# Layer 2's mixing matrix S: one row part from 32-column matmuls, the other from the copies out of PSUM

## The chip, the cores and the metric

One Trainium2 chip, one core. The metric is the device time of the kernel in microseconds (us). TensorE's trace has two rows, PE for matmuls and PEld for weight loads; DVE is VectorE, ACT is ScalarE, POOL is GpSimd, SP is the engine that issues most DMAs.

## The reference

The input x has 16 samples of 16 channels of 256x256 fp32 pixels. Four layers follow each other, each of the form x = x + layer(groupnorm(x)): a circular 3x3 convolution, a 5x5 convolution with a diagonal kernel, a pole-residue layer, and a quantised 3x3 convolution. Only the third, layer 2, is touched:

```
alpha = fft2(x)
A  = 1 / (omega1 - weights_pole1)          Bm = 1 / (omega2 - weights_pole2)
S  = einsum('ikpq,oikp,xikq->oxik', weights_residue, A, Bm)
output_residue1 = einsum('biox,oxik->bkox', alpha, S)
x1 = real(ifft2(output_residue1))          # x2, a second term, comes from the same poles
return x1 + x2 / Nx / Ny
```

For every frequency pair (o, x) a complex 16x16 matrix S mixes the channels i of alpha into the channels k of the result. In real numbers that is a 32x32 matrix: the rows for the real part of alpha hold (Re S, Im S), the rows for the imaginary part hold (-Im S, Re S). These two groups of rows are the two row parts.

## The kernel before

The program runs in stages. Layers 0 and 1 take about the first 1,300 us. The next stage (to about 2,240 us) transforms each sample and stores alpha to DRAM (`alphad`). Then comes the stage of this document, about 2,240 to 3,100 us: S is made and multiplied with alpha, and the product goes to DRAM (`mixd`). The inverse transform (to about 3,970 us) reads `mixd`, and layer 3 ends the program.

In the mixing stage four frequencies o share one matmul. The tile `z` holds, on 128 partitions, the rows of alpha of four frequencies f, and in its columns a block for each f, zero elsewhere. The tile `sk` holds S for the same four: for each of 129 positions x a 128x32 stationary matrix. One product is `sk[:, x]` (128x32) against `z[:, :, x]` (128x64), written to one of four groups of 32 PSUM partitions (L958). Sixty-four rounds n (`NF`) of 129 products follow each other. In a round, the loop over `at` runs 32 times with four products each; every eighth `at` closes a PSUM tile `ps_m`, which ScalarE copies in part to `other` (L983) and VectorE adds and subtracts into `ob` (two operations recorded at the helper's line L190). `ob` is stored to `mixd` (`leave`, L911) and `z` for a later round is loaded from `alphad` (`load`, L907, sixteen partitions to a DMA), both on SP's queue.

`system(e8)` makes S for eight frequencies, two rounds' worth, in eight steps of two channels k. A step works through both halves h of the input channels. For each it multiplies `l` (`ls[h]`, 128x128: the factor A, masked; its columns are 8 frequencies, 2 row parts, 8 channels) with `t2[:, h, k]` (128x258: the sum over q of residue and Bm, the two parts interleaved with x) for two k into a tile `ps_s` (L891), and copies the two frequency halves n of that tile into two `sk` tiles, 64 partitions each, on ScalarE (L896). Thus a step is four matmuls and four copies. `masked` makes `l` on GpSimd, four operations for two steps; `poles` makes `af`, the factor A with both row parts, on GpSimd and VectorE once for eight steps.

The order of the work is written out by hand in this stage (`manual_schedule` for PE, DVE, ACT and POOL): the engines take their instructions in the order in which the code issues them. `next(steps)` issues one step at each eighth `at`, so a step and 32 products alternate, four times in a round. The eight steps of `system(0)` come before the first product; 248 of the 256 steps lie between products, and the last two rounds have none. `ps_s` has two buffers, `ps_m` three, `sk` four.

Of the kernel before, what the change touches and what calls it, by code (L numbers as in the profile page):

```python
# [57 lines left out]
P = 128  # L58
C = 16
# [12 lines left out]
def constants():  # L72
# [10 lines left out]
    def sin(a, b):  # L83
# [81 lines left out]
def layers(ctx, tc, x, w0, w1, w3, sw, bias, ty, tx, p1a, p1b, p1c, p2a, p2b, p2c, resa, resb,  # L165
# [23 lines left out]
    def tt(eng, o, a, b, op):  # L189
        eng.tensor_tensor(o, a, b, op)  # L190
# [368 lines left out]

    between = ExitStack()  # L560
    late2 = between.enter_context(tc.tile_pool(name="late2", bufs=1))
    t2 = new(late2, [HC, C, NX, 2], "t2")
# [5 lines left out]
    def sums_over_q(pool, psum):  # L568
# [32 lines left out]
        for h in range(HC):  # L601
            for k0 in range(0, C, KQ):
                e, g = new(pool, [KQ, NX], "qe"), new(pool, [KQ, NX], "qg")
                of = lambda c: bc(c[:, h, k0 : k0 + KQ], 2, NX)
                tt(Q, e, bc(wx, 1, KQ), of(pxi), SUB)
                nc.scalar.activation(g, e, AF.Square)
                tt(Q, g, g, of(px2), ADD)
                yield
                V.reciprocal(g, g)
                yield  # L610
                V.scalar_tensor_tensor(e, e, turn[:, 2:3], of(pxr), MUL, ADD)
                tt(V, e, e, g, MUL)
                w = new(pool, [2 * KQ, 2, 8, 8], "qw")
                c0 = h * C + k0
                for v in range(2):
                    tt(Q, w[:, :, v], bc(cf[:, c0 : c0 + KQ].rearrange("p n (m r) q -> p (n m) (r q)", m=2), 3, 8),
                       bc(bc(vi[:, v], 1, 8), 1, 2 * KQ), MUL)
                yield
                for k in range(KQ):
                    ps = psum.tile([P, 512], F32, tag="ps_a", name="ps_t")  # L620
                    for m in range(2):
                        nc.tensor.matmul(ps[:, m * NX : (m + 1) * NX], start=m == 0, stop=m == 1, rhs=e[:, k],
                                         lhsT=w[:, 2 * k + m].rearrange("p v r i -> p (v r i)"), skip_group_check=True)
                    nc.scalar.copy(t2[:, h, k0 + k].rearrange("p x r -> p r x"),
                                   ps[:, 0 : 2 * NX].rearrange("p (r x) -> p r x", r=2))
# [5 lines left out]
        Q.tensor_scalar(t2[:, :, :, 0, 0], t2[:, :, :, 0, 1], -1.0, None, MUL)  # L631
        Q.tensor_copy(t2[:, :, :, 0, 1], a)
        yield

    afs, lss, sks = {}, {}, {}
# [5 lines left out]
    def poles(e8, pool=None, psum=None):  # L641


        af = afs[e8] = new(head, [HC, 2, C, FC], f"af{e8 % 2}")
        if pool:
            e, d = new(pool, [HC, C, FC], "ae"), new(pool, [HC, C, FC], "ad")
        else:
            e, d = (new(head, [KC, FC, 2, 8], f"l{h}1").rearrange("p k f r i -> p (k f r i)")[:, 0 : HC * C * FC]
                    .rearrange("p (h k f) -> p h k f", h=HC, k=C) for h in range(HC))
        g = psum.tile([P, HC, C, FC], F32, tag="ps_g", name="ps_g") if psum else d  # L650
        for h in range(HC):
            tt(Q, e[:, h], bc(wy[:, FC * e8 : FC * e8 + FC], 1, C), bc(pyi[:, h], 2, FC), SUB)
        yield
        tt(Q, d, e, e, MUL)
        yield
        tt(Q, d, d, bc(py2, 3, FC), ADD)
        yield
        V.reciprocal(g, d)
        yield
        eng = V if psum else Q  # L660
        for k, at in enumerate(blocks):
            tt(eng, af[at, :, 1 - k % 2], e[at], g[at], MUL)
            yield
            tt(eng, af[at, :, k % 2], g[at], bc(pyr, 3, FC)[at], MUL)
            yield

    def masked(e8, k0):

        if e8 == NE:
            return  # L670
        ls = []
        for h in range(HC):
            l = new(head, [KC, FC, 2, 8], f"l{h}{k0 // KC % 2}")
# [3 lines left out]
            ls.append(l.rearrange("p k f r i -> p k (f r i)"))  # L677
        lss[e8, k0] = ls


    with ExitStack() as es:
# [77 lines left out]
        rows2 = alphad.rearrange("(p s) h r i q x b -> p s h r i q (x b)", s=2)  # L759
        es.enter_context(tc.manual_schedule(engines={mybir.EngineType.PE}))  # L760

        def quarters(b, g):
# [26 lines left out]
        def across(b, i, y, al, acc):  # L789
# [13 lines left out]
            V.scalar_tensor_tensor(flat(al[:, 1, :, :, b % BG]), pc, not0, sums[1], MUL, SUB)  # L803
            if b % BG == BG - 1:
                for s_, eng in enumerate((nc.sync, Q)):
                    eng.dma_start(rows2[:, s_, i // 8, :, i % 8, b // BG, :],
                                  al[:, s_].rearrange("p r x b -> p r (x b)"))

            ps = ps_d.tile([P, P], F32, tag="ps_d", name="ps_d")
# [56 lines left out]
    with ExitStack() as es:  # L866
# [12 lines left out]
        def system(e8):  # L879


            for n in range(2):
                sks[2 * e8 + n] = new(sp, [NX, 2 * C], "sk")
            for k0 in range(0, C, KC):
                masked(*((e8, k0 + KC) if k0 + KC < C else (e8 + 1, 0)))
                ls = lss.pop((e8, k0))
                for k in range(k0, k0 + KC, 2):
                    for h in range(HC):
                        ps = ps_s.tile([P, 2, 512], F32, tag="ps_s", name="ps_s")
                        for d in range(2):  # L890
                            nc.tensor.matmul(ps[:, d, 0 : 2 * NX], lhsT=ls[h][:, k + d - k0],  # L891
                                             rhs=t2[:, h, k + d].rearrange("p x r -> p (x r)"), start=True, stop=True)
                            if d:
                                for n in range(2):
                                    copy = V.tensor_copy if e8 == 0 and n and h else nc.scalar.copy
                                    copy(sks[2 * e8 + n][64 * h : 64 * h + 64, :, 2 * k : 2 * k + 4]  # L896
                                         .rearrange("p x (k r) -> p x k r", r=2),
                                         ps[64 * n : 64 * n + 64, :, 0 : 2 * NX].rearrange("p k (x r) -> p x k r", r=2))
                    yield

        PX = 32
        GX = 8

        def load(n, h, f, to):

            rows_ = slice(64 * h + 16 * f, 64 * h + 16 * f + 16)
            nc.sync.dma_start(zs[n % 2][rows_, 4 * to : 4 * to + 4].rearrange("p q x b -> p (q x b)"),  # L907
                              alphad[4 * n + f, h].rearrange("r i q x b -> (r i) (q x b)"))

        def leave(n, p_):  # L910
            nc.sync.dma_start(mixd[2 * n + p_].rearrange("t k r u b g -> (t k r) (u b g)"),  # L911
                              obs[n][:, p_].rearrange("p u b g -> p (u b g)"))

        def halfload(n, h):

            if n < NF:
                z = zs[n % 2]
                for f in range(4):
                    V.memset(z[64 * h : 64 * h + 64, 4 * f, 0, 0:1], 0.0)
                    load(n, h, f, f)  # L920

# [8 lines left out]
        for _ in range(3):  # L930
            next(coming)
        Q.memset(zs[0][:, FB // 2 :], 0.0)
        for h in range(HC):
            for f in range(4):
                for to in ((0, 1) if f < 2 else (f,)):
                    load(0, h, f, to)
        for at, _ in enumerate(system(0)):
            for _ in range(2):
                next(coming, None)
# [78 lines left out]
    with ExitStack() as es:  # L1018
# [99 lines left out]
        with tc.manual_schedule(engines={mybir.EngineType.PE}):  # L1118
            before = None
            exps = exponentials(0)  # L1120
            for k in range(0, C, 2):
                for b in range(B):
                    if b % BD == 0:

                        ot = op.tile([P, 2, 2, 4, 2, BD, 32], F32, tag="ot", name="ot")
                        for a in range(2):
                            for d in range(2):
                                for r in range(2):
                                    for u in range(2):
                                        nc.sync.dma_start(  # L1130
                                            ot[64 * u : 64 * u + 64, a, d, :, r].rearrange("p t b g -> p t (b g)"),
                                            mixd[64 * a : 64 * a + 64, :, k + d, (r + u) % 2, u, b : b + BD]
                                            .rearrange("q t b g -> q t (b g)"))
                    if b == 4:
                        coming = exponentials(k + 2) if k + 2 < C else None
# [271 lines left out]
```

## Time and profile before

| what | value |
|---|---|
| three timed runs | 4389.43, 4389.74 and 4402.79 us, median 4389.74 us |
| the profiled execution's own time, first to last instruction (its span) | 4393.6 us, 3.9 us over the median |
| PE busy over the span | 3976.0 us (90%) |
| DVE, ACT, POOL busy over the span | 69%, 63%, 48% |
| mixing with steps, from 2276 to 3069 us: PE, ACT, POOL, DVE busy of 793 us | 756, 668, 504, 420 us |
| DMA in that stretch | mean busy share 0.74, 167 GB/s |
| `z` loads, `mixd` stores: issues, KB each, median us to landing | 516, 129.0, 4.8; 128, 512.0, 5.9 |

Busy time of an engine is the time in which one of its instructions runs; matmuls are pipelined and their ends are modelled, so PE's share counts starts more safely than ends. A fp32 matmul shows as two instructions, so the 1,024 matmuls of S are 2,048 in the profile. An operation recorded through the helper at L190 is told apart by its tiles.

### The profile page before, as it was taken

Reading aid. Unit: us, or ns where it says so; the run is one execution under the profiler, and the core shown is the slowest. Engines: PE = TensorE matmul, PEld = TensorE weight load, DVE = VectorE, ACT = ScalarE, POOL = GpSimd, SP = SyncE. Lnnn points to the kernel's source line nnn. Section 1 sums busy time; section 2 is a strip of 40 time slices with the busy share of each in tenths; the row PEclk is TensorE's granted clock in tenths of the full one; section 3 lists DMA queues with packets and bytes.
Section 4 is the critical chain, followed back from the end, with each engine's and each line's share of the span. In section 5 each row is a group of like instructions: output and inputs, shape, how many; then the busy total and the mean of one; then the engine's idle time right before and its main releaser. Section 6 shows DMA issues by size and latency. Waiting matters only on the chain. (4 is left out here: it accounts for less than half of the span.)

```text
span 4393.6 us, 122873 instructions
## 1 busy us (share of the span) xinstructions
PE 3976.0 (90%) x50832; PEld 3066.8 (70%) x50832; DVE 3037.6 (69%) x5678; ACT 2753.7 (63%) x3699; POOL 2125.9 (48%) x3350
## 2 busy tenths in 40 slices
PE   5999999999958989899989999999799999996776
PEld 1555555555538989899977777777588888884444
DVE  4667677666668878787755555554477777768988
ACT  2877676868624434444458888888555544446998
POOL 2242323333245646564556666665476666663222
PEclk9999999999979999999999999999799999998999
DMA  6767676767443545344547777777788888877998
GB/s 147 168 166 181 156 184 148 192 143 193 111 124 115 164 133 164 121 159 150 169 89 163 164 172 167 172 174 166 209 228 235 231 244 234 244 219 257 357 351 306
DMA packets 481647, 820.57 MB, mean 187 GB/s; under 512 B 41728, under 2 KB 373504, under 8 KB 465664
## 3 DMA queue, kind: packets, MB, share of 16 engines
q1 hardware_dynamic: 433984, 644.64, 54.8%
q0 software_dynamic: 47104, 168.06, 12.8%
q8 instruction: 401, 6.57, 0.7%
q14 instruction: 158, 1.29, 0.1%
HBM read 408.85 MB, written 336.07 MB: 170 GB/s over the span
## 5 line engine op out<-in xcount | busy, mean ns | idle before, releaser
L382 PE MATMUL ps<-va,wt 128*64 128x512 f32 (+1 forms) x1632 | 667.8, 570 | 11.4 <-POOL va L354 9.2
L382 PE MATMUL ps<-vb,wt 128*64 128x512 f32 (+1 forms) x1632 | 666.0, 569 | 4.5 <-DMA vb<-va 4.5
L896 ACT COPY sk<-ps_s 64x516 f32<-64x516 f32 x1016 | 592.3, 583 | 115.6 <-PE ps_s L891 96.3
L786 ACT ACTIVATE y<-ps_y,bc 128x384 f32<-128x384 f32 x512 | 296.0, 580 | 406.3 <-PE ps_y L784 406.2
L891 PE MATMUL ps_s<-t,l 128*128 128x258 f32 x2048 | 523.8, 398 | 17.1 <-ACT sk L896 7.5
L190 DVE TENSOR_TENSOR ob<-ps_m,other 128x256 f32<-128x256 f32 x512 | 270.8, 606 | 352.3 <-ACT other L983 347.6
L403 ACT ACTIVATE v<-xt,nm 32x2048 f32<-32x2048 f32 x248 | 497.1, 2004 | 9.7 <-PE ps L417 3.5
L417 PE MATMUL ps<-v,w1s 128*64 128x259 f32 x4096 | 481.1, 394 | 11.0 <-DVE v L401 6.7
L190 POOL TENSOR_TENSOR w<-rq 128x512 f32<-128x512 f32 x256 | 334.7, 1328 | 261.0 <-ACT rq L1097 260.2
L382 PEld LDWEIGHTS ps<-va,wt 128*64 128x64 f32 x1632 | 222.9, 137 | 311.5 <-issue 283.4
L891 PEld LDWEIGHTS ps_s<-t,l 128*128 128x128 f32 x2048 | 371.8, 192 | 95.5 <-issue 9.6
L417 PEld LDWEIGHTS ps<-v,w1s 128*64 128x64 f32 x4096 | 336.6, 141 | 133.1 <-issue 23.8
L1096 PE MATMUL ps_o<-exp,fs 128*128 128x128 f32 x2048 | 399.9, 277 | 12.0 <-ACT fs L1144 11.9
L1095 PE MATMUL ps_o<-c_last,zt 128*128 128x128 f32 x2048 | 398.6, 277 | 0.0
L1241 PE MATMUL ps_c<-q,wt 64*64 64x512 bf16 (+1 forms) x4608 | 290.2, 402 | 102.7 <-ACT o L1288 85.4
L1095 PEld LDWEIGHTS ps_o<-c_last,zt 128*128 128x128 f32 x2048 | 323.6, 193 | 60.8 <-issue 60.8
L958 PEld LDWEIGHTS ps_m<-z,sk 128*32 128x32 f32 x16384 | 254.1, 110 | 123.8 <-issue 102.9
L190 POOL TENSOR_TENSOR acc<-acc,prod 128x256 f32<-128x256 f32 x240 | 232.6, 969 | 221.9 <-DVE prod L190 215.5
L958 PE MATMUL ps_m<-z,sk 128*32 128x64 f32 x16384 | 302.2, 223 | 36.6 <-issue 33.9
L1241 PEld LDWEIGHTS <-wt 64*64 64x64 bf16 x4800 | 180.2, 113 | 212.7 <-issue 144.2
L1096 PEld LDWEIGHTS ps_o<-exp,fs 128*128 128x128 f32 x2048 | 313.8, 194 | 13.8 <-ACT fs L1144 13.8
L781 PE MATMUL ps_y<-c_y,qd 128*128 128x128 f32 x2048 | 314.6, 276 | 1.9 <-ACT hat L743 1.8
(356 smaller groups left out, 8748.8 us busy)
## 6 DMA issues: line engine op xcount, KB each, us to landing
xt<-x2d SPq DMA_DIRECT2D x256, 512.0 KB, 4.3
z<-alphad SPq DMA_DIRECT2D x516, 129.0 KB, 4.8
xt<-in_x_dram SPq DMA_DIRECT2D x256, 256.0 KB, 7.4
x2d<-x2s POOLq DMA_DIRECT2D x256, 256.0 KB, 5.0
mixd<-ob SPq DMA_DIRECT2D x128, 512.0 KB, 5.9
ot<-mixd SPq DMA_DIRECT2D x256, 256.0 KB, 6.2
x3d<-xt SPq DMA_DIRECT2D x128, 512.0 KB, 5.4
xt<-x3d SPq DMA_DIRECT2D x64, 1024.0 KB, 8.3
```

The lines of the kernel that those rows point to most:

```text
L190: eng.tensor_tensor(o, a, b, op)
L382: nc.tensor.matmul(ps[halves[h], lo:hi, :], lhsT=wt0[:, w, :], rhs=v[:, 2 * t + lo : 2 * t + hi, j : j + N], start=j == 0 and k == 0, stop ...
L403: nc.scalar.activation(to, o.xt[c][q_], AF.Identity, bias=o.g.nm[q_, 1:2])
L417: nc.tensor.matmul(ps[halves[h], k, 0:U], lhsT=o.w1[:, w : w + 64], rhs=v1[:, lo : lo + U], start=first_, stop=not first_)
L781: nc.tensor.matmul(to[:, :, a, :], lhsT=v[:, c, a, i % 2, :], start=a == 0, stop=a == 1, rhs=y1[:, a].rearrange("p (r f) -> p r f", r=2))
L786: nc.scalar.activation(y[:, c, :], ps[:, 0 : 3 * P], AF.Copy, scale=bc2[:, b, i // 2, 0:1])
L891: nc.tensor.matmul(ps[:, d, 0 : 2 * NX], lhsT=ls[h][:, k + d - k0], rhs=t2[:, h, k + d].rearrange("p x r -> p (x r)"), start=True, stop=True)
L896: copy(sks[2 * e8 + n][64 * h : 64 * h + 64, :, 2 * k : 2 * k + 4] .rearrange("p x (k r) -> p x k r", r=2), ps[64 * n : 64 * n + 64, :, 0 ...
L958: nc.tensor.matmul(to, lhsT=sk[:, x_], rhs=z[:, :, x_], start=True, stop=True)
L1095: nc.tensor.matmul(ps[:, a, c, :], lhsT=zts[d][:, a, c, :], rhs=last[:, c, :], start=True, stop=False)
L1096: nc.tensor.matmul(ps[:, a, c, :], lhsT=fs[:, d, a, :], rhs=ey[:, d, c, :], start=False, stop=True)
L1241: nc.tensor.matmul(o, lhsT=wt[half[h], w, :], rhs=src, start=i == 0, stop=i == len(work[0]) - 1)
```

## The change

S's second row part is no longer multiplied out. `af` and `l` lose the row-part axis: `l` has 32 columns for each half n of the frequencies (8 channels x 4 frequencies), and a step makes eight matmuls of 128x32 against 128x258, into four groups of 32 partitions of a single `ps_s` tile for both h. Then, for n = 1 and n = 0 in turn, three operations read 64 partitions of PSUM: one copies both parts to the first 64 partitions of `sk`, one copies Re S and one copies -Im S, swapped, to the last 64. The first is always ScalarE's; the other two are VectorE's for n = 1 and ScalarE's for n = 0. `sk`'s rows are now (row part, h, channel, frequency), so the rows of one frequency are every fourth partition: a `z` load is one DMA of 32 partitions with a step of four in place of two of 16 neighbours. `alphad` and `mixd` are laid out to match, with as many bytes and rows of the same length. `t2` keeps its two parts apart, so that the copy that fills it is contiguous. `poles` has one last multiplication for all partitions where it had eight on 32, and two GpSimd copies ahead of it.

```diff
-    f4 = p // 16 % 4
+    f4 = p % 4
...
-        "imag": 1.0 * (p % 2 == 1), "real": 1.0 * (p % 2 == 0),
+        "imag": 1.0 * (p // C % 2 == 1), "real": 1.0 * (p // C % 2 == 0),
...
-    mixd = dram.tile([N // 2, 4, C, 2, 2, B, 32], F32, tag="mixd", name="mixd")
+    mixd = dram.tile([N // 2, 4, 2, C, 2, B, 32], F32, tag="mixd", name="mixd")
...
-        eng = V if psum else Q
-        for k, at in enumerate(blocks):
-            tt(eng, af[at, :, 1 - k % 2], e[at], g[at], MUL)
+        for at in blocks[0::2]:
+            Q.tensor_copy(e[at], bc(pyr, 3, FC)[at])
             yield
-            tt(eng, af[at, :, k % 2], g[at], bc(pyr, 3, FC)[at], MUL)
-            yield
+        tt(V if psum else Q, af, e, g, MUL)
+        yield
...
-            l = new(head, [KC, FC, 2, 8], f"l{h}{k0 // KC % 2}")
-            for r in range(2):
-                a = afs[e8][:, h, r, k0 : k0 + KC]
-                tt(Q, l[:, :, :, r], bc(a, 3, 8), bc(bc(mod, 1, FC), 1, KC), MUL)
+            l = new(head, [KC, 2, 8, 4], f"l{h}{k0 // KC % 2}")
+            a = afs[e8][:, h, k0 : k0 + KC].rearrange("p k (n f) -> p (k n) f", n=2)
+            tt(Q, l.rearrange("p k n i f -> p (k n) i f"), bc(a, 2, 8), bc(bc(mod, 1, 2 * KC), 3, 4), MUL)
...
-                    for h in range(HC):
-                        ps = ps_s.tile([P, 2, 512], F32, tag="ps_s", name="ps_s")
-                        for d in range(2):
-                            nc.tensor.matmul(ps[:, d, 0 : 2 * NX], lhsT=ls[h][:, k + d - k0],
-                                             rhs=t2[:, h, k + d].rearrange("p x r -> p (x r)"), start=True, stop=True)
-                            if d:
-                                for n in range(2):
-                                    copy = V.tensor_copy if e8 == 0 and n and h else nc.scalar.copy
-                                    copy(sks[2 * e8 + n][64 * h : 64 * h + 64, :, 2 * k : 2 * k + 4]
-                                         .rearrange("p x (k r) -> p x k r", r=2),
-                                         ps[64 * n : 64 * n + 64, :, 0 : 2 * NX].rearrange("p k (x r) -> p x k r", r=2))
+                    ps = ps_s.tile([P, 2, 512], F32, tag="ps_s", name="ps_s")
+                    for d in range(2):
+                        for n in range(2):
+                            for h in range(HC):
+                                at = 64 * n + 32 * h
+                                nc.tensor.matmul(ps[at : at + 32, d, 0 : 2 * NX], lhsT=ls[h][:, k + d - k0, n],
+                                                 rhs=t2[:, h, k + d].rearrange("p r x -> p (r x)"), start=True, stop=True)
+                    for n in (1, 0):
+                        from_ = ps[64 * n : 64 * n + 64, :, 0 : 2 * NX].rearrange("p k (r x) -> p x r k", r=2)
+                        to = sks[2 * e8 + n].rearrange("p x (r k) -> p x r k", r=2)[:, :, :, k : k + 2]
+                        nc.scalar.copy(to[0:64], from_)
+                        if n:
+                            V.tensor_copy(to[64:P, :, 1], from_[:, :, 0])
+                            V.tensor_scalar(to[64:P, :, 0], from_[:, :, 1], -1.0, None, MUL)
+                        else:
+                            nc.scalar.copy(to[64:P, :, 1], from_[:, :, 0])
+                            nc.scalar.mul(to[64:P, :, 0], from_[:, :, 1], -1.0)
                     yield
...
-        def load(n, h, f, to):
+        quads4 = [slice(f, P, 4) for f in range(4)]
...
-            rows_ = slice(64 * h + 16 * f, 64 * h + 16 * f + 16)
-            nc.sync.dma_start(zs[n % 2][rows_, 4 * to : 4 * to + 4].rearrange("p q x b -> p (q x b)"),
-                              alphad[4 * n + f, h].rearrange("r i q x b -> (r i) (q x b)"))
+            nc.sync.dma_start(zs[n % 2][quads4[f], 4 * to : 4 * to + 4].rearrange("p q x b -> p (q x b)"),
+                              alphad[4 * n + f].rearrange("r h i q x b -> (r h i) (q x b)"))
```

In the changed program's instruction order, a step on ScalarE and VectorE and the groups of products beside it stand as follows. The tags name the engine that an instruction waits for; the waits on ScalarE's second copy reach to the negation (`L897`) of the same step.

```
ACT  L983 other<-ps_m          [waits PE, ACT]
ACT  L894 sk<-ps_s  n = 1      [waits PE]
ACT  L894 sk<-ps_s  n = 0      [waits DVE]
ACT  L899 sk<-ps_s, L900 sk<-ps_s
DVE  L190 ob<-ps_m,other x2    [waits ACT]
DVE  L896 sk<-ps_s  n = 1      [waits ACT]
DVE  L897 sk<-ps_s  n = 1
```

More of the change, by code (lines that the diff above doesn't have):

```diff
@@ L561, in layers @@
     late2 = between.enter_context(tc.tile_pool(name="late2", bufs=1))
-    t2 = new(late2, [HC, C, NX, 2], "t2")
+    t2 = new(late2, [HC, C, 2, NX], "t2")
     wy = new(late2, [N], "wy")
@@ L623, in sums_over_q @@
                                          lhsT=w[:, 2 * k + m].rearrange("p v r i -> p (v r i)"), skip_group_check=True)
-                    nc.scalar.copy(t2[:, h, k0 + k].rearrange("p x r -> p r x"),
-                                   ps[:, 0 : 2 * NX].rearrange("p (r x) -> p r x", r=2))
+                    nc.scalar.copy(t2[:, h, k0 + k].rearrange("p r x -> p (r x)"), ps[:, 0 : 2 * NX])
                     if k % 2:
@@ L630, in sums_over_q @@
         Q.tensor_copy(a, t2[:, :, :, 0, 0])
-        Q.tensor_scalar(t2[:, :, :, 0, 0], t2[:, :, :, 0, 1], -1.0, None, MUL)
-        Q.tensor_copy(t2[:, :, :, 0, 1], a)
+        Q.tensor_scalar(t2[:, :, :, 0, 0], t2[:, :, :, 1, 0], -1.0, None, MUL)
+        Q.tensor_copy(t2[:, :, :, 1, 0], a)
         yield
@@ L641, in poles @@
     def poles(e8, pool=None, psum=None):
-        af = afs[e8] = new(head, [HC, 2, C, FC], f"af{e8 % 2}")
+        af = afs[e8] = new(head, [HC, C, FC], f"af{e8 % 2}")
         if pool:
@@ L647, in poles @@
         else:
-            e, d = (new(head, [KC, FC, 2, 8], f"l{h}1").rearrange("p k f r i -> p (k f r i)")[:, 0 : HC * C * FC]
-                    .rearrange("p (h k f) -> p h k f", h=HC, k=C) for h in range(HC))
+            e, d = (new(head, [HC, C, FC], f"l{h}1") for h in range(HC))
         g = psum.tile([P, HC, C, FC], F32, tag="ps_g", name="ps_g") if psum else d
@@ L758, in layers @@
         qp = es.enter_context(tc.tile_pool(name="b_q", bufs=1))
-        rows2 = alphad.rearrange("(p s) h r i q x b -> p s h r i q (x b)", s=2)
+        rows2 = alphad.rearrange("(p s) r h i q x b -> p s r h i q (x b)", s=2)
         es.enter_context(tc.manual_schedule(engines={mybir.EngineType.PE}))
@@ L805, in across @@
                 for s_, eng in enumerate((nc.sync, Q)):
-                    eng.dma_start(rows2[:, s_, i // 8, :, i % 8, b // BG, :],
+                    eng.dma_start(rows2[:, s_, :, i // 8, i % 8, b // BG, :],
                                   al[:, s_].rearrange("p r x b -> p r (x b)"))
@@ L916, in halfload @@
             if n < NF:
[L917 to L920, printed above, removed]
+                for f in (2 * h, 2 * h + 1):
+                    V.memset(zs[n % 2][:, 4 * f, 0, 0:1], 0.0)
+                    load(n, f, f)
         es.enter_context(tc.manual_schedule(engines={
@@ L932, in layers @@
         Q.memset(zs[0][:, FB // 2 :], 0.0)
[L933 to L936, printed above, removed]
+        for f in range(4):
+            for to in ((0, 1) if f < 2 else (f,)):
+                load(0, f, to)
         for at, _ in enumerate(system(0)):
@@ L1131, in layers @@
                                             ot[64 * u : 64 * u + 64, a, d, :, r].rearrange("p t b g -> p t (b g)"),
-                                            mixd[64 * a : 64 * a + 64, :, k + d, (r + u) % 2, u, b : b + BD]
+                                            mixd[64 * a : 64 * a + 64, :, (r + u) % 2, k + d, u, b : b + BD]
                                             .rearrange("q t b g -> q t (b g)"))
```

5 lines of the change are left out of this document (3 added, 2 removed).

## The prediction

> **What bounds the kernel now.** I read the page's shares first, then its costliest groups, then the mixing stage alone.
>
> ```profile
> PE 3976.0 (90%) x50832; PEld 3066.8 (70%) x50832; DVE 3037.6 (69%) x5678; ACT 2753.7 (63%) x3699; POOL 2125.9 (48%) x3350
> ...
> L896 ACT COPY sk<-ps_s 64x516 f32<-64x516 f32 x1016 | 592.3, 583 | 115.6 <-PE ps_s L891 96.3
> ...
> L891 PE MATMUL ps_s<-t,l 128*128 128x258 f32 x2048 | 523.8, 398 | 17.1 <-ACT sk L896 7.5
> ```
>
> TensorE is the busiest engine of the span, but the kernel is a chain of stages. Two groups of the page belong to the step that the change rewrites: ScalarE's copies out of PSUM (583 ns each) and TensorE's matmuls of S. The table by stretches puts them in their stage; its columns are start and end, length, busy us of PE, PEld, DVE, ACT and POOL with instructions, then granted clock, DMA share and GB/s.
>
> ```profile
> 2276.00:3069.00 793.00, 756.05 (x17952) 599.16 (x17955) 419.52 (x1326) 668.02 (x1236) 503.80 (x1106) 1.00 0.74 167
> ...
> 3900.00:4393.00 493.00, 366.84 (x5890) 246.80 (x5882) 423.70 (x473) 398.24 (x347) 148.87 (x140) 0.90 0.85 306
> ```
>
> In the 793 us from the first product to the last copy of S, TensorE is busy for 95%, ScalarE for 84%. These 793 us hold 248 steps: 3.20 us each. The waits inside the stage name the loser (engine, line, whom it waited for; us in total, times, longest).
>
> ```profile
> DVE ob L190 <- ACT other L983: 322.8, 211, 6.2
> ...
> ACT sk L896 <- PE ps_s L891: 77.1, 236, 3.8
> ```
>
> VectorE waits for ScalarE's `other` 323 us long, and ScalarE waits for TensorE. So TensorE leads, ScalarE follows at a short distance, and VectorE idles. The timeline of one step shows the handovers: first ScalarE, then VectorE (start, length, what; in brackets the idle time before).
>
> ```profile
> 2703.51 0.37 ACT L983 COPY other<-ps_m 128x256 f32<-128x256 f32 x1
> 2704.07 2.38 ACT L896 COPY sk<-ps_s 64x516 f32<-64x516 f32 x4 [0.20 <-PE ps_s L891]
> 2706.48 0.37 ACT L983 COPY other<-ps_m 128x256 f32<-128x256 f32 x1
> ```
>
> ```profile
> 2703.91 1.07 DVE L190 TENSOR_TENSOR ob<-ps_m,other 128x256 f32<-128x256 f32 x2 [0.99 <-ACT other L983]
> 2705.04 0.08 DVE L919 MEMSET z<- 64x1 f32 x4
> 2706.88 0.60 DVE L190 TENSOR_TENSOR ob<-ps_m,other 128x256 f32<-128x256 f32 x1 [1.76 <-ACT other L983]
> ```
>
> A clean step takes 2.97 us, from one `other` to the next; the 0.23 us up to 3.20 are lost mostly at the ends of rounds. ScalarE's `other` ends at 2703.88, and VectorE starts `ob` at 2703.91: a handover costs 0.03 us. The pair of `ob` takes 1.07 us. Then VectorE has 1.76 us of slack up to the next pair.
>
> **TensorE's part.** The products already run as the new S will: four groups of 32 columns.
>
> ```profile
> L958 PE MATMUL ps_m<-z,sk x16384: 216/219/317, 2276.0 to 3088.2; 128*32 128x64 f32 x200
> ```
>
> In the timeline at 2750 us the step's eight instructions of S take 2.01 us and the 64 instructions of its products 1.04 us. That is 1.04/(64 x 64) = 0.25 ns for a column of a product, against 2.01/(8 x 258) = 0.97 ns for one of S. The new step has sixteen instructions of 258 columns: 16 x 258 x 0.25 = 1.05 us. TensorE's step falls from 3.05 to about 2.1 us. This alone would remove the bound, so what counts is who is late next.
>
> **The new copies, one by one.** ScalarE has per step, before, 4 x 0.583 + 0.372 = 2.70 us. After, it has two copies of 64x516 and two operations of 64x258. Their rows:
>
> ```profile
> L786 ACT ACTIVATE y<-ps_y,bc 128x384 f32<-128x384 f32 x512 | 296.0, 580 | 406.3 <-PE ps_y L784 406.2
> ...
> L800 ACT COPY pc<-ps_a 128x258 f32<-128x258 f32 x256 | 94.2, 368 | 49.7 <-PE ps_a L795 49.7
> ...
> L624 ACT COPY t<-ps_t 128x258 f32<-128x258 f32 x32 | 12.9, 403 | 18.9 <-PE ps_t L622 18.2
> ```
>
> A contiguous read of 258 is 0.368 us, and writing every second word makes it 0.403; I take 0.39 for L899. The multiplication by -1 is an ACTIVATE: 580 ns at 384 elements here and 693 at 518 (L424) give 0.84 ns an element, so 0.474 us at 258. VectorE's two have these rows:
>
> ```profile
> L426 DVE TENSOR_SCALAR x2s<-ps,gm 128x518 f32<-128x518 f32 x144 | 109.0, 757 | 104.1 <-PE ps L417 102.4 <-DMA x2d<-x2s 1.7
> ...
> L190 DVE TENSOR_TENSOR af<-ps_g,pyr 32x256 f32<-32x256 f32 x124 | 51.2, 413 | 0.1
> ...
> L896 DVE COPY sk<-ps_s 64x516 f32<-64x516 f32 x8 | 5.6, 699 | 11.4 <-ACT sk L896 11.3
> ```
>
> L896 with 699 ns at 516, and the 292 ns of a 128x128 copy (L829), give 1.05 ns an element: 0.428 us for 258. The tensor_scalar is 757 - 260 x 1.05 = 484 ns. Two operations on the same partitions overlap by 0.07 us (`af` pairs of 413 and 417 ns start 0.345 us apart), so the pair takes 0.84 us.
>
> **The wait that it adds.** ScalarE's copy for n = 0 waits for VectorE's negation for n = 1 of the same step, and VectorE's copy for n = 1 waits for ScalarE's first copy. VectorE takes instructions in the order written: the `ob` pair of group k stands ahead of its two operations of step k+1, and that pair waits for `other` of group k. Behind the waiting n = 0 copy stand ScalarE's L899, L900 and `other` of group k+1, and for that `other` the next `ob` waits. So there is a loop between the two engines in which nothing overlaps:
>
> - `other` 0.37, handover 0.03;
> - the `ob` pair 1.07, and 0.03 before an operation on other partitions starts (`ob` to `af` shows that gap): 1.10;
> - VectorE's copy and negation 0.84, handover back 0.03;
> - ScalarE's n = 0 copy 0.595 (583 ns and 12 ns between copies), L899 0.40, L900 0.49: 1.49.
>
> Sum: 0.37 + 0.03 + 1.10 + 0.84 + 0.03 + 1.49 = 3.86 us. ScalarE's first copy (0.58, after 0.20 of gap) hides beside the `ob` pair. TensorE's 2.1 us hide too: two `ps_s` buffers let it run a step ahead. So 248 steps take 957 us in place of 793: 164 us more.
>
> The bounds of that loop. Below: `ob` to a reciprocal starts with 0.15 us of overlap, so the gap of 0.03 could be -0.15; and ACTIVATEs overlap their neighbours by 0.10 in the stage before (L786 to L800), twice 0.2 us in sum. That makes 3.48 us, and 70 us more. Above: each of the four new operations and the n = 0 copy writes pairs 64 bytes apart and could cost 0.036 more, as L624 does over L800 (0.18); and the 0.23 us at round ends could stay. That makes 4.27 us, and 266 us more. I take the middle sum, since its gaps come from rows of this stage with the same kind of operation.
>
> **The rest.** VectorE's other work (the reciprocal of 1.73 us, one `af` of 0.42 in place of eight, memsets, `alone_`) stands between the negation and the next `ob`, where VectorE waits 0.03 + 1.49 + 0.37 + 0.03 = 1.92 us: covered. Without that cover the 1.73 us come once in eight steps, 0.22 a step, within the upper bound. GpSimd loses two of four masks (617 ns each) per two steps, gains two copies of 32x256 per eight, and has 36% to spare: nothing. The `z` loads become 258 of 258 KB in place of 516; SP issues fewer, and TensorE waited 2.2 us for them in all, so faster ones give nothing and longer rounds give them more time. `mixd` and `alphad` keep their row lengths; TensorE waits 33.6 us for `ot` in the inverse stage, and I bound a change of DRAM order by half of that both ways, taken at 0. `t2`'s 32 copies save 0.035 us each behind TensorE: 0. The eight steps of `system(0)` have the loop without `ob` and `other`: 0.58 + 0.03 + 0.84 + 0.03 + 1.49 = 2.97 us, 24 us against 28 now, of which VectorE's work on `z` keeps some: 0.
>
> Sum: the profiled execution has 4393.6 us, 3.9 over the median; 4393.6 + 164 = 4557.6, on the median's footing 4389.7 + 164 = 4554 us.
>
> **Two rules of the Trainium skill.** VectorE's start 0.03 us after `other` shows that such waits are obeyed and how short a handover is. "PSUM — Partial Sum Buffer", section "PSUM bank collisions raise a hardware error", says that two engines may use one bank at once in different quarters of 32 partitions; the n = 0 copy reads partitions 0 to 63 and VectorE 64 to 127, so by the rule the wait is not needed, and the time would be that of the first rival. The instruction order has the wait, so I do not use it. The clock: 1.00 is granted at 95% busy, 0.90 in the last stage at 74%. The new stage has TensorE at 2.1 of 3.86 us, lower than any row; were its clock halved, its 4.2 us a step would exceed the loop by 0.3 us, 84 us more than forecast. "TensorE: Matmul & The Clock Gate", section "What's actually happening", wants an idle window of about 3.4 us for the slow clock; pauses here are below 2 us, so by it nothing.
>
> **Rivals.** *The wait decides nothing* (faster): ScalarE's own work is then the bound, 0.583 + 0.20 + 0.595 + 0.40 + 0.49 + 0.37 = 2.64 us, 655 us for 248 steps, 138 less: 4252 us. For it: TensorE's relief is certain by the products' row. Against it: the order of the instructions. It decides below 3.20 us a step, so 0.66 us of my 3.86 would have to lie beside other work; I can find 0.38. *Strided reads of PSUM at half rate*: the new copies read no two neighbours; 516 + 258 + 258 elements x 0.83 ns on ScalarE and 516 x 1.05 on VectorE add 1.40 us to the loop, 347 us to the forecast: 4901. Against it: the old copies read pairs, and 583 ns at 516 is what a contiguous 128x512 takes (587, L1097). *The four column groups do not overlap* (the change does not do what it says): sixteen instructions at 0.25 us and the products are 5.06 us, 1255 us, 462 more than now: 4852. Against it: the products' row.
>
> **How the numbers follow.** A serial loop of 3.48 to 4.27 us: 0.81, at 4554. The wait decides nothing: 0.07. Half-rate reads 0.04, no overlap 0.04. A loop within 0.05 us of 3.20: 0.04. The median of the runs tells differences over 0.3%. Faster 0.07, same 0.04, slower 0.89. The range of the loop is 4460 to 4656; leaving out its two ends and the rivals, 4465 to 4650 keeps 8 in 10.
>
> **What would show it.** Right: VectorE's waits for ScalarE's `other` stay, ScalarE waits for VectorE's `sk` some 240 times, TensorE near 55% busy, `other` every 3.5 to 4.3 us. Wrong: ScalarE busy above 90% in the stage with `other` every 2.7 us; L894 or L899 far above 583 and 403 ns; TensorE still above 90%.

## The result and the profile after

The changed kernel takes 4560.55 us (median of 4 runs, 4555.49 to 4562.98) against 4390.68 us before (4 runs, 4389.43 to 4402.79). The ratio is 1.038, with a 95% interval of 1.0358 to 1.0402: slower by 3.8%. The forecast was 4554 us, 4465 to 4650. The profiled execution has a span of 4553.7 us against 4393.6.

The page's shares, the two groups that were read before, and the mixing stage in the table by stretches (start and end, length, busy us of PE, PEld, DVE, ACT and POOL, granted clock, DMA share, GB/s):

```profile
PE 3834.6 (84%) x52880; PEld 2914.3 (64%) x52880; DVE 3157.3 (69%) x5713; ACT 2635.1 (58%) x3707; POOL 1999.2 (44%) x3151
...
L894 ACT COPY sk<-ps_s 64x516 f32<-64x516 f32 x512 | 306.5, 599 | 416.4 <-DVE sk L897 402.5
...
L889 PE MATMUL ps_s<-t,l 128*32 128x258 f32 x4096 | 340.6, 456 | 233.6 <-ACT sk L900 181.9
```

```profile
2276.00:3240.00 964.00, 623.77 (x20130) 458.97 (x20126) 541.26 (x1371) 550.97 (x1242) 381.10 (x925) 0.85 0.41 139
```

TensorE fell from 95% of the stage to 65%, ScalarE from 84% to 57%. No engine is near its limit, and yet the stage is longer: a loop of waits. ScalarE's copy used to idle for TensorE; it now idles 402.5 us for VectorE's `sk`. The waits of the stage after (2300 to 3150 us; us in total, times, longest) show both halves of the loop at the top, and near them a wait that the prediction did not have, the last line.

```profile
ACT sk L894 <- DVE sk L897: 348.2, 219, 3.5
DVE ob L190 <- ACT other L983: 264.9, 165, 1.7
PE ps_s L889 <- ACT sk L900: 152.5, 97, 3.8
PEld ps_s L889 <- issue: 142.7, 167, 4.0
DVE af L190 <- POOL ae L659: 91.2, 27, 3.4
```

One turn of the loop, on ScalarE and then on VectorE:

```profile
2706.46 0.37 ACT L983 COPY other<-ps_m 128x256 f32<-128x256 f32 x1
2706.86 0.61 ACT L894 COPY sk<-ps_s 64x516 f32<-64x516 f32 x1
2708.75 0.58 ACT L894 COPY sk<-ps_s 64x516 f32<-64x516 f32 x1 [1.28 <-DVE sk L897]
2709.34 0.37 ACT L899 COPY sk<-ps_s 64x258 f32<-64x258 f32 x1
2709.61 0.38 ACT L900 ACTIVATE sk<-ps_s 64x258 f32<-64x258 f32 x1
2710.02 0.37 ACT L983 COPY other<-ps_m 128x256 f32<-128x256 f32 x1
```

```profile
2706.86 1.06 DVE L190 TENSOR_TENSOR ob<-ps_m,other 128x256 f32<-128x256 f32 x2 [1.71 <-ACT other L983]
2707.94 0.43 DVE L896 COPY sk<-ps_s 64x258 f32<-64x258 f32 x1
2708.29 0.42 DVE L897 TENSOR_SCALAR sk<-ps_s 64x258 f32<-64x258 f32 x1
```

Follow the starts: `other` 2706.46, `ob` 2706.86, VectorE's copy 2707.94, ScalarE's second L894 at 2708.75, L899 at 2709.34, the next `other` at 2710.02. Where the engine changes, each begins 0.03 to 0.04 us after the end of what it waits for. One turn is 3.56 us; before, a clean step took 2.97.

The time from the first `other` to the 248th went from 792.7 to 955.3 us, 162.6 more. The start of the stage moved by 2.2 us, and all that follows it got 4.7 us shorter, which gives the 160.1 us between the two spans. The change is wholly in these steps. Their mean is 3.87 us, where 3.86 was forecast, but they are not alike. The table has the median time from one `other` to the next by place in eight steps (two rounds), from the trace, with the mean of 247 behind it, for all the kernels that follow:

| kernel | 1 | 2 | 3 | 4 | 5 | 6 | 7 | 8 | mean |
|---|---|---|---|---|---|---|---|---|---|
| before | 2.98 | 3.07 | 2.98 | 2.97 | 2.97 | 3.06 | 3.41 | 2.98 | 3.21 |
| after | 3.73 | 5.75 | 3.54 | 3.59 | 3.59 | 3.62 | 3.56 | 3.58 | 3.87 |
| e1_scalar_first | 2.19 | 2.84 | 3.36 | 4.97 | 2.56 | 2.25 | 2.81 | 3.21 | 3.24 |
| e2_copies_early | 4.05 | 3.62 | 3.61 | 3.59 | 3.57 | 3.60 | 3.60 | 3.58 | 3.65 |
| e3_both | 2.19 | 3.17 | 3.43 | 3.27 | 2.80 | 2.78 | 2.77 | 2.75 | 3.04 |
| e4_all_scalar | 2.99 | 2.97 | 3.02 | 3.00 | 2.97 | 3.00 | 2.97 | 3.00 | 3.00 |
| e5_fewer_instr | 2.17 | 3.15 | 2.74 | 4.16 | 2.19 | 2.25 | 2.16 | 3.83 | 2.84 |
| e6_late_alone | 2.27 | 3.15 | 3.60 | 2.84 | 2.72 | 2.73 | 2.84 | 2.73 | 2.95 |
| e7_late_fewer | 2.53 | 2.77 | 2.80 | 2.21 | 2.20 | 2.25 | 2.20 | 2.22 | 2.48 |
| e8_before_fewer | 2.95 | 3.04 | 2.95 | 2.95 | 2.95 | 3.05 | 2.95 | 2.95 | 2.99 |
| e9_after_fewer | 3.72 | 5.75 | 3.56 | 3.58 | 3.55 | 3.62 | 3.55 | 3.56 | 3.86 |
| e10_one_moved | 2.57 | 2.58 | 3.65 | 3.14 | 2.61 | 2.62 | 2.77 | 2.61 | 2.98 |

After has 3.5 to 3.7 us in seven places and 5.75 in the second. There, first VectorE's and then GpSimd's operations:

```profile
2716.02 0.21 DVE L992 COPY alone__25375<-ps_e 32x64 f32<-32x64 f32 x1
2719.62 0.42 DVE L190 TENSOR_TENSOR af<-ae,ps_g 128x256 f32<-128x256 f32 x1 [3.39 <-POOL ae L659]
2719.96 1.02 DVE L190 TENSOR_TENSOR ob<-ps_m,other 128x256 f32<-128x256 f32 x2
```

```profile
2716.32 0.24 POOL L190 TENSOR_TENSOR e<-alone__25375 32x32 f32<-32x32 f32 x1 [6.86 <-DVE alone__25375 L992]
...
2718.88 0.27 POOL L190 TENSOR_TENSOR ob<-ob,e 32x32 f32<-32x32 f32 x1
2719.20 0.39 POOL L659 COPY ae<-pyr 32x256 f32<-32x256 f32 x1
```

`af` needs GpSimd's new copies of `pyr` (L659). The last of them is queued on GpSimd behind eight small operations on `alone_`, and those waited 6.86 us for VectorE's copy of `alone_` at 2716.02. So VectorE stands still for 3.39 us with the `ob` pair queued behind `af`. That `ob` belongs to the loop, and 2.1 us of the stall reach it.

### The profile page after: what moved, and what is told of

Its sections match the earlier page's. It is cut to its first block, busy times and chain, and to the rows that moved or that the text cites. A ratio compares the mean times of both kernels' runs of the same rounds, so it can differ in the third digit from the quotient of the medians.

```text
span 4553.7 us, 126254 instructions
## 1 busy us (share of the span) xinstructions
PE 3834.6 (84%) x52880; PEld 2914.3 (64%) x52880; DVE 3157.3 (69%) x5713; ACT 2635.1 (58%) x3707; POOL 1999.2 (44%) x3151
## 5 line engine op out<-in xcount | busy, mean ns | idle before, releaser
L894 ACT COPY sk<-ps_s 64x516 f32<-64x516 f32 x512 | 306.5, 599 | 416.4 <-DVE sk L897 402.5
L889 PE MATMUL ps_s<-t,l 128*32 128x258 f32 x4096 | 340.6, 456 | 233.6 <-ACT sk L900 181.9
L958 PEld LDWEIGHTS ps_m<-z,sk 128*32 128x32 f32 x16384 | 336.2, 126 | 200.7 <-ACT sk L900 93.4
L958 PE MATMUL ps_m<-z,sk 128*32 128x64 f32 x16384 | 360.3, 247 | 118.5 <-ACT sk L900 77.8
L889 PEld LDWEIGHTS ps_s<-t,l 128*32 128x32 f32 x4096 | 138.9, 126 | 323.0 <-issue 167.6
```

Source lines behind the costliest of these rows:

```text
L889: nc.tensor.matmul(ps[at : at + 32, d, 0 : 2 * NX], lhsT=ls[h][:, k + d - k0, n], rhs=t2[:, h, k + d].rearrange("p r x -> p (r x)"), start ...
L894: nc.scalar.copy(to[0:64], from_)
L958: nc.tensor.matmul(to, lhsT=sk[:, x_], rhs=z[:, :, x_], start=True, stop=True)
```

## The experiments

**Two causes, taken apart.** The theory was the loop (3.6 us a step) plus this standstill of VectorE, the stall, once in eight steps. The rival was that the stall is harmless and the step is 3.86 us by itself. Four kernels ran together, beside 13 runs of before with a median of 4397.05 us.

e1_scalar_first turns the order round, so that ScalarE's three operations for n = 0 come first and none of ScalarE's copies waits for VectorE's of the same step:

```diff
-                    for n in (1, 0):
+                    for n in (0, 1):
```

> The changed kernel with one edit: the copies out of PSUM are issued for n = 0 first and n = 1 second, so that ScalarE's three operations for n = 0 no longer stand behind VectorE's two for n = 1. The same operations, the same matmuls. Theory (a loop between ScalarE and VectorE sets the step, 3.6 us clean, plus one stall of VectorE behind GpSimd's copy of pyr, 2.1 us once in eight steps): the loop is gone, ScalarE's own work is 2.28 us a step by the changed kernel's rows, VectorE's 1.9 and 0.7 for what comes once in eight steps, the stall included. 2.6 to 2.75 us a step, 4250 to 4290 us. Rival A (the new copies cost what they cost: strided reads, more operations on two engines, no loop): the same operations, so 4540 to 4580 us. Rival B (TensorE sets the pace at its lower granted clock, 0.85 in the stage): TensorE's work is untouched, so 4540 to 4580 us.

Measured: 4398.33 us, ratio 1.0003 (0.9991 to 1.0015), 162 us less than after by the medians. Practically the whole loss is gone with one line. ScalarE in the middle of a round, with no wait at all:

```profile
2708.08 0.37 ACT L983 COPY other<-ps_m 128x256 f32<-128x256 f32 x1
2708.35 0.60 ACT L894 COPY sk<-ps_s 64x516 f32<-64x516 f32 x1
2708.96 0.37 ACT L899 COPY sk<-ps_s 64x258 f32<-64x258 f32 x1
2709.23 0.38 ACT L900 ACTIVATE sk<-ps_s 64x258 f32<-64x258 f32 x1
2709.64 0.59 ACT L894 COPY sk<-ps_s 64x516 f32<-64x516 f32 x1
2710.25 0.37 ACT L983 COPY other<-ps_m 128x256 f32<-128x256 f32 x1
```

This step takes 2.17 us with the same operations, so the loop came from the order of the copies. But the kernel missed the expected 4250 to 4290 us: the mean step is 3.24, and only two places of eight come near 2.2. Something else is late next.

e2_copies_early leaves the order and moves GpSimd's two copies ahead of the reciprocal. At each `yield` other work is let in, and with the two copies their yields go, so that VectorE's multiplication for `af` comes sooner after the reciprocal:

```diff
         tt(Q, d, d, bc(py2, 3, FC), ADD)
+        for at in blocks[0::2]:
+            Q.tensor_copy(e[at], bc(pyr, 3, FC)[at])
         yield
         V.reciprocal(g, d)
         yield
-        for at in blocks[0::2]:
-            Q.tensor_copy(e[at], bc(pyr, 3, FC)[at])
-            yield
```

> The changed kernel with one edit: in poles, GpSimd's two copies of pyr are issued directly after the addition of py2, ahead of the reciprocal, so that VectorE's last multiplication for af does not wait for them behind GpSimd's work on alone_. Theory: the long step in eight (5.7 us against 3.6) falls to 3.6, but the multiplication now stands beside the reciprocal in one step, whose 1.75 + 0.43 and memsets exceed VectorE's 1.7 us of slack by 0.5. 31 x (2.1 - 0.5) = 50 us less: 4500 to 4520 us, and every step still at 3.6. Rival A and B (copies or clock set the pace, the stall is covered): 4550 to 4570 us.

Measured: 4506.9 us, ratio 1.0247 (1.0226 to 1.0267), as expected. The second place fell from 5.75 to 3.62 us; the mean by 0.218 us, and 247 x 0.218 = 54 us is the whole difference to after. So the stall is real and moving the copies is worth 54 us, and the loop alone is 3.6 us a step.

e3_both has both edits.

> The changed kernel with both edits: copies for n = 0 first, and GpSimd's copies of pyr ahead of the reciprocal. Theory: no loop and no stall; ScalarE 2.28, VectorE 1.9 + 0.3, TensorE 2.15 us a step at full clock, close together. 2.35 to 2.55 us a step, 4190 to 4240 us, which is under the kernel before. Rival A: as the second edit alone, 4500 us or more. Rival B: TensorE at 0.85 of its clock needs 2.5 us, so 4220 to 4260 if the clock stays low, and 4540 if it is what holds the changed kernel.

Measured: 4353.96 us, ratio 0.9897 (0.9879 to 0.9915). It is 1% faster than before, but missed 4190 to 4240 by far. The mean step is 3.04 us where its undisturbed steps take 2.2.

e4_all_scalar keeps after's order and gives all six copies to ScalarE:

```diff
-                        if n:
-                            V.tensor_copy(to[64:P, :, 1], from_[:, :, 0])
-                            V.tensor_scalar(to[64:P, :, 0], from_[:, :, 1], -1.0, None, MUL)
-                        else:
-                            nc.scalar.copy(to[64:P, :, 1], from_[:, :, 0])
-                            nc.scalar.mul(to[64:P, :, 0], from_[:, :, 1], -1.0)
+                        nc.scalar.copy(to[64:P, :, 1], from_[:, :, 0])
+                        nc.scalar.mul(to[64:P, :, 0], from_[:, :, 1], -1.0)
```

> The changed kernel with VectorE's two operations for n = 1 given to ScalarE, so that all six copies of a step are ScalarE's. Theory: ScalarE has more work, 2.28 + 0.67 = 2.95 us a step and up to 0.2 of gap, but waits for VectorE no more: 2.95 to 3.15 us, 4330 to 4390 us, so faster than the changed kernel by moving work to its busier engine. Rival A: ScalarE has 0.67 us a step more and VectorE less; with ScalarE's work as the bound, slower than the changed kernel or the same, 4560 to 4730 us. Rival B: the same, 4540 to 4580 us.

Measured: 4344.37 us, ratio 0.9879 (0.986 to 0.9899), as expected. ScalarE is the bound here, 97% busy (its row of 2300 to 2900 us):

```profile
2300.00:2900.00 600.00, 427.68 (x16130) 314.05 (x16122) 268.52 (x700) 582.72 (x1403) 309.42 (x753) 0.99 0.54 180
```

More work on ScalarE is 216 us faster than work shared with VectorE in the wrong order: without the waits between the two engines loop and stall are both gone (all eight places take 3.0 us), and that is worth more than the work that ScalarE gains.

**What holds e3_both.** Its waits, 2300 to 3000 us:

```profile
PEld ps_m L957 <- issue: 166.0, 124, 3.4
...
PE ps_m L957 <- issue: 106.2, 75, 3.2
...
PEld ps_s L888 <- POOL l L190: 35.8, 46, 2.5
```

"issue" means that the profile shows nothing that TensorE waits for. The trace does show something else: DMA transfers of 16 KB on the queue of TensorE's instructions, one for 255.7 instructions (38096 over 149, weight loads and semaphore instructions included). A typical pause, on PE:

```profile
2717.79 0.61 PE L957 MATMUL ps_m<-z,sk 128*32 128x64 f32 x27
2720.03 0.58 PE L957 MATMUL ps_m<-z,sk 128*32 128x64 f32 x26 [1.62 <-issue]
```

Such a transfer ran from 2717.61 to 2718.57, and TensorE went on 1.46 us after its end. Of e3_both's 132 pauses over 0.3 us in these 700 us, 95 end 1.2 to 1.7 us after such a transfer has ended, 133 us in all (the expectations below say 91). So do all 32 pauses over 0.3 us of before, at 1.2 to 1.9 us. Theory A: TensorE runs out of instructions. Theory B: GpSimd's order and the z loads. To tell them apart, e5_fewer_instr streams the same columns through TensorE with 48 matmul instructions a step in place of 80, and with as many fewer weight loads:

```diff
+            def double(to, x_):
+                nc.tensor.matmul(to.rearrange("p x (f b) -> p x f b", f=FB), lhsT=sk[:, x_],
+                                 rhs=z[:, :, x_ : x_ + 2].rearrange("p f x b -> p x f b"), start=True, stop=True)
...
-                for a in range(4):
-                    product(ps[32 * a : 32 * a + 32, at % GX], 1 + PX * a + at)
+                for a in range(0 if at % 2 else 4):
+                    double(ps[32 * a : 32 * a + 32, at % GX : at % GX + 2], 1 + PX * a + at)
```

> e3_both, with TensorE's products of two neighbouring positions made by one instruction of 128 columns in place of two of 64 (the second position gets the first one's weights, so the output is not the reference's). TensorE streams as many columns as before and every other instruction stays; its instructions fall from 80 matmuls a step to 48. Theory A: e3_both is held up by TensorE's supply of instructions. In e3_both, 91 of TensorE's 132 pauses over 0.3 us, 133 us of the 700 us looked at, end 1.2 to 1.7 us after a 16 KB transfer of instructions has landed. By A about 0.44 us a step goes, 248 x 0.44 = 110 us: 4245 us (4215 to 4290), and such pauses nearly vanish. Theory B: GpSimd's order and the loads of z hold it up, and the instruction transfers only stand nearby: 4354 us (4335 to 4370).

e6_late_alone moves GpSimd's operations on `alone_`:

```diff
+                if at == 2 * GX:
                     for u, (op_, new_, old) in enumerate(((ADD, imag, real), (SUB, real, imag))):
```

> e3_both, with GpSimd's eight small operations on alone_ and ob issued one and two steps later (at position 16 in place of 8), so that GpSimd does not stand 6.8 us at the head of its queue for VectorE's copy before it makes the next masks l. TensorE's waits for GpSimd's l, 55 us of 700 in e3_both, should go. Theory B (GpSimd's order sets the step): the step falls to about 2.3 us, 4180 us (4150 to 4230). Theory A (TensorE's supply of instructions): at most those 55 us of 700 go, 19 us of the stage's 248 steps: 4335 us (4320 to 4360).

e7_late_fewer has both of these edits, and e8_before_fewer is before with the joined products.

> e5_fewer_instr and e6_late_alone together (output as in e5_fewer_instr). If A and B each hold a part: below both, about 4200 us (4150 to 4240), with a step of 2.2 to 2.5 us, near the 2.19 us of e3_both's undisturbed steps. If a third cause holds the stage, such as the loads of z: about as e5_fewer_instr.

> The kernel before, with the products joined in pairs as in e5_fewer_instr (its output is not the reference's for the same reason); TensorE's matmuls fall from 72 to 40 a step and its columns stay. All 32 of TensorE's pauses over 0.3 us in the 700 us of before end 1.2 to 2 us after an instruction transfer: 29 us, 10 to 11 ns of each us. Theory A: these go, 793 x 29/700 = 33 us less: 4360 us (4350 to 4375). Rival: the pauses at round ends belong to the z loads and to the order of the round: no change, 4395 us (4385 to 4405).

Measured together, beside 7 runs of before with a median of 4392.39 us:

| kernel | us | ratio | 95% interval |
|---|---|---|---|
| e5_fewer_instr | 4298.08 | 0.9779 | 0.9751 to 0.9806 |
| e6_late_alone | 4330.67 | 0.985 | 0.9821 to 0.9879 |
| e7_late_fewer | 4205.78 | 0.9562 | 0.9527 to 0.9597 |
| e8_before_fewer | 4343.79 | 0.988 | 0.9853 to 0.9907 |

e8_before_fewer is the cleanest case: 49 us less, with nothing changed but how many instructions, matmuls and weight loads, make TensorE's products. All 32 pauses after transfers are gone, and a single pause over 0.3 us is left, which follows no transfer in this way. The gain is 16 us more than the 33 us expected. About 6 of them are the undisturbed step, 2.95 us in place of 2.97; shorter pauses hold only 2 us of 700 in before, and the rest stays open. Its page's DMA queue line (before: 401 transfers, 6.57 MB), and the stretch from 2300 to 2900 us of before and of e8_before_fewer:

```profile
q8 instruction: 337, 5.52, 0.6%
```

```profile
2300.00:2900.00 600.00, 572.78 (x13569) 453.90 (x13571) 322.71 (x1012) 506.10 (x937) 379.73 (x844) 0.99 0.75 168
```

```profile
2300.00:2900.00 600.00, 598.66 (x8144) 457.36 (x8144) 343.18 (x1083) 544.71 (x1007) 410.58 (x908) 1.00 0.82 180
```

TensorE is now busy for nearly all of it, 598.66 of 600 us. The whole program has 8,192 matmul instructions and 8,192 weight loads fewer than before, and 64 transfers fewer: one for 256 instructions.

e5_fewer_instr fell between the two expectations, 8 us above A's range. Its pauses after transfers went from 133 to 9 us in 700, as A said, but half of the gain was lost. The next wait in line is that for GpSimd's masks, which e3_both shows with 35.8 us for weight loads and 18.9 for matmuls in 700 us. Here, in only 600:

```profile
PEld ps_s L888 <- POOL l L190: 130.3, 132, 2.0
...
PE ps_s L888 <- POOL l L190: 77.7, 47, 1.7
```

e6_late_alone takes those waits away (2.5 us in 700 are left) and gains little, as A expected, since the pauses after transfers stay (150 us in 700). By the ratios, from e3_both's 0.9897, the first edit alone gains 1.2% of before's time, the second alone 0.5%, and both together 3.4%, twice the sum: while either cause is there, it hides most of what the other costs. In e7_late_fewer five of eight places take 2.2 us; VectorE and ScalarE are 89% busy (516 of 580 us) and near their limits:

```profile
2300.00:2880.00 580.00, 488.20 (x11513) 353.74 (x11509) 516.41 (x1300) 516.18 (x1184) 362.26 (x877) 0.99 0.65 217
```

**A control and a last version**, beside 7 runs of before with a median of 4396.7 us. e9_after_fewer is the changed kernel with the joined products.

> The changed kernel with the products joined in pairs as in e5_fewer_instr (output as there). In the changed kernel TensorE's pauses that end 1.2 to 1.7 us after a transfer of instructions are only 35 of 700 us, and most of its pauses are waits for ScalarE's copies. Theory A (the loop between ScalarE and VectorE sets the changed kernel's step, TensorE waits for it): no change, 4555 us (4540 to 4570). Rival (TensorE's supply of instructions lengthens the step here too, as in the kernel before and in e3_both): 48 us or more less, 4510 us or below.

Measured: 4554.05 us, ratio 1.0358 (1.0326 to 1.039), against 1.038 (1.0358 to 1.0402) for after: no difference clear of noise. The same edit that gains 1.2% in before and in e3_both gains nothing that shows here, so TensorE's instructions are off the path in the changed kernel.

e10_one_moved is e6_late_alone with one of VectorE's two copies back on ScalarE:

```diff
                         if n:
-                            V.tensor_copy(to[64:P, :, 1], from_[:, :, 0])
+                            nc.scalar.copy(to[64:P, :, 1], from_[:, :, 0])
                             V.tensor_scalar(to[64:P, :, 0], from_[:, :, 1], -1.0, None, MUL)
```

> e6_late_alone with only the negation for n = 1 on VectorE; its plain copy goes back to ScalarE. ScalarE's work a step is e4_all_scalar's 2.97 us less one multiplication (0.38): 2.6 us; the two engines hand over once a step less. If the waits between the two engines cost e6_late_alone more than ScalarE's extra 0.37 us: about 2.75 us a step, the pace of TensorE's supply of instructions, 248 x 0.2 = 50 us less: 4280 us (4260 to 4320), the fastest version with the full work. If ScalarE's own work and TensorE's supply add up instead: as e4_all_scalar and e6_late_alone, 4335 us (4320 to 4350).

Measured: 4337.43 us, ratio 0.986 (0.9834 to 0.9887): the second expectation. Five places take about 2.6 us, ScalarE's own work, but the pauses after transfers (134 us in 700) stay, and the mean is 2.98. I read this as the two adding up, since ScalarE has no slack left to catch up with; no run separates them. e6_late_alone has the lowest time of the kernels that do the whole work, 1.5% under before and 5% under after, but its interval overlaps those of e10_one_moved and e4_all_scalar.

## Why the prediction was right, and where it was not

The side, the mechanism and the time were right. The time was right in part by luck: two errors of 0.26 us a step cancelled.

- **The loop.** Right, and shown by e1_scalar_first, where one swapped line takes the loss away. By its terms, from the turn shown above: `other` and handover 0.40 forecast, 0.40 measured; the `ob` pair with its gap 1.10 and 1.08; VectorE's copy, negation and the handover 0.87 and 0.81 (the negation takes 0.42, not 0.48); the n = 0 copy 0.595 and 0.59; L899 and L900 0.89 and 0.68. This last term failed. The ACTIVATE takes 377 ns, where rows of 384 and 518 elements had given 474 by extrapolation, and it starts 0.10 us before L899 ends. I had seen that overlap and put it into the lower bound alone. The loop is 3.56 us in the turn shown, 3.60 as the median of all 247, not 3.86.
- **"Covered", the step that failed.** VectorE's other work had 1.92 us of slack, and I asked whether it fits. I did not ask whom it waits for. Of GpSimd's two new copies I counted the time, 36% spare, and not the place in the queue: behind operations that wait for VectorE itself. That is 2.1 us once in eight steps; without it the mean step falls by 0.22 us (e2_copies_early). The reciprocal is not fully covered either: the first place takes 3.73 us in the changed kernel, and 4.05 in e2_copies_early, where the multiplication stands close behind it; e2_copies_early's mean is still 0.05 above 3.60. Together this is about the 0.26 by which the forecast loop was too long.
- **TensorE's part.** Right: sixteen instructions of S take 1.08 us where they run in one go (forecast 1.05), and TensorE stays off the path (e9_after_fewer). It is busy for 65% of the stage, not near 55%: at the mean granted clock of 0.85, 2.1 us of work would take about 2.5 us of the 3.87, an estimate that fits.
- **The 0.23 us "lost mostly at the ends of rounds"** in before was for the most part TensorE's supply of instructions: in e8_before_fewer the seventh place falls from 3.41 to 2.95 us and the mean by 0.22.
- **z loads, mixing order, `system(0)`: nothing.** Right. A z load of 258 KB lands in 3.1 us where 129 KB took 4.8, and no gain comes from it, as the stage's length is the loop's. Outside the steps the two spans differ by 2.5 us: 2.2 more ahead of them, 4.7 less behind them.
- **The rivals.** That the wait decides nothing is refuted by e1_scalar_first, and its price does not hold for any kernel tried that does the whole work: without the loop these took 4331 to 4398 us, not 4252. I had made ScalarE's own work the next bound, and it was TensorE's instructions and GpSimd's queue; with both eased, and its products joined, e7_late_fewer took 4206. Half-rate reads: refuted by 592 ns for L894 and 430 for L896 (forecast 583 and 428). No overlap of column groups: refuted by the 1.08 us.
- **The clock.** The step's pauses were to be below 2 us and the clock unaffected. TensorE's pauses reached 3.8 us, and the granted clock of the stage was 0.85. A lower clock is not what lengthened the step: e1_scalar_first and then e2_copies_early, from 2300 to 2900 us, have nearly the same clock, and steps of 3.24 and 3.65 us on average.

```profile
2300.00:2900.00 600.00, 426.44 (x14881) 334.33 (x14885) 401.99 (x1017) 405.72 (x924) 283.01 (x691) 0.89 0.51 166
```

```profile
2300.00:2900.00 600.00, 384.43 (x13214) 283.19 (x13218) 361.37 (x904) 365.17 (x824) 255.24 (x620) 0.91 0.43 147
```

## What to carry to other kernels

When a change shares one buffer's copies between two engines, write down both queues and look for a cycle: a wait in each direction per step can make the two engines work as one, and here the order of two loop iterations cost 162 us, more than twice the 62 us that the best version here gained over before. Of an operation said to be covered, ask not only how long it takes but whom it waits for and what stands ahead of that in its queue. After the bound is lifted, expect several waits that hide one another: price them together, since each alone recovered 0.5% or 1.2% and both 3.4%.

## What the runs showed of the hardware

**Instructions have to be fetched, and TensorE can outrun it.** In before, one transfer of 16 KB comes for 255.2 of TensorE's instructions (32406 over 127), and pauses end 1.2 to 1.9 us after one. The Trainium skill, "Runtime: NRT & Kernel Launch", section "Instruction fetch mechanics", states blocks of 16 KiB for 256 instructions, which agrees, and calls the cost of crossing such a block mostly hidden. Here the pauses after transfers were 29 of 700 us in before, where fewer instructions saved 49 of 4392 us (1.2% by the ratio), and 133 of 700 us in e3_both; the measurement decides. Why some transfers come in time and others late stays open: the transfer itself took 0.88 to 1.4 us in most cases of e3_both, and its start was not varied by any run.

**The clock drops at half-idle stretches.** In after the granted clock is 0.5 for stretches of 3.4 or 6.8 us, 181 of the 600 us from 2300 to 2900. The Trainium skill, "TensorE: Matmul & The Clock Gate", section "What's actually happening", ties the halved clock to an idle window of about 3.4 us. In e2_copies_early no pause of TensorE is over 2.5 us, and still 113 of 600 us ran at 0.5. Cut the time from 2300 to 2900 us into windows of 3.41 us in step with these stretches. In before, after and e2_copies_early, full clock followed only windows of which TensorE spent 0.53 or less idle; each of e3_both's 15 windows at half clock and e4_all_scalar's 2 followed one with 0.56 or more. Between the two, 0.53 to 0.59, both occurred. So a window need not be wholly idle: half clock came after 0.56. No run here varied this alone.
